# Strassen's scheme for the features of token blocks 0 and 1 in a float32 attention and gated-FFN kernel

## The chip, the cores and the metric

The kernel runs on one core of one Trainium2 chip. The metric is device time in microseconds (us) of one execution; a median of several executions is given. TensorE (PE) multiplies matrices and loads stationary operands beside it (PEld); VectorE (DVE), ScalarE (ACT) and GpSimd (POOL) work on tiles in SBUF; SyncE (SP) issues most of the DMA transfers, ACT some.

## The reference

Two sequences of 2048 tokens, 2048 channels, float32. Each token is normalised; from the normalised x come q, k, v (512 each), the router's q (16) and the bottleneck z (64 experts x 8):

```python
xn  = (x - mean) / sqrt(var + 1e-5)
q, k, v = split(xn @ Wqkv + bqkv)                    # 2048 -> 3 x 512
att = softmax(q @ k.T / sqrt(512)) @ v               # per sequence
gate = scatter(softmax(top_16(xn @ Wq.T @ keys.T)))  # 64 experts
z   = (xn @ A.T).reshape(.., 64, 8) * gate[..., None]
out = x + att @ Wo + bo + 2 * z.reshape(.., 512) @ B.T
```

## The kernel before

Every product of float32 matrices is made of three passes: each operand is split into a rounded high part (`split_hi`, line 126, ACT) and the rest (`split_lo`, line 129, DVE), and `product` (line 132) runs low x high, high x low, high x high.

The 4096 tokens are eight blocks of T = 512; two blocks make a pair. First all blocks get their "features" (12 tiles of 128 rows: q, k and z, made with weights stationary and x moving, 128x512) and their "values" (v and the router's 16 columns, in two halves of VH = 264 columns, x stationary and weights moving, 128x264). Then come scores, softmax and values (lines 1154 to 1316), then the output product (line 1466).

Blocks 0 and 1 are computed directly. `first_block` (line 336) loads block 0's rows, normalises, turns and splits them, and makes its values. `ftile` (line 548) makes one of block 0's 12 feature tiles: 16 chunks of channels x 3 passes = 48 matmuls. Then `values` (line 313) and 12 more calls of `ftile` do block 1; `norm` (line 261) normalises its x, which comes turned from memory (`xT`). Row statistics of the next blocks (`stats_steps`, line 212) run beside.

Pairs 1, 2 and 3 use a scheme of Strassen's kind: for a pair, the two blocks are the columns, the two halves of channels the inner dimension and the two halves of features the rows of a 2 x 2 product, which takes seven products of half size instead of eight. The products are the phases P1, P2, P6, P5, P3, P7, P4 (`phase`, line 801), each six feature pieces of 8 chunks x 3 passes = 24 matmuls and a value piece. P1 + P2 is the first block's first half; the others need sums of x (`sum_steps`, line 673) and sums of weights (`four_sums`, line 572, four GpSimd instructions), which are made once, beside the features of blocks 0 and 1, and stored in DRAM (`sq_d` for features, `sv_d` for values).

The weights of a piece are fetched by `fetch` (line 619) two pieces ahead: a load by SP into one of three buffers (`r_pw`), a high part on ACT and a low part on DVE into one of three pairs (`r_ph`). Results go to DRAM through `store` and `flush` (line 167), on SP's queue.

Each engine takes its instructions in a fixed order, which a planner lays down when the program is built. `behind(...)` holds a step's place in that order behind a named instruction. An SP transfer whose data isn't ready holds up the transfers behind it.

Of the kernel before, what the change touches and what calls it, by code (L numbers as in the profile page):

```python
# [62 lines left out]
def attn_ffn_kernel(ctx: ExitStack, tc, x, xT, wq, wv, wob, bqk, bv, bo, keysT, out):  # L63
# [68 lines left out]
    def product(ps, st, mv, first, end):  # L132

        for n, (a_, b_) in enumerate(PASSES):
            last["pe"] = nc.tensor.matmul(  # L135
                ps, st(a_), mv(b_), start=first and n == 0, stop=end and n == 2
            )
# [35 lines left out]
    r_xh = big(*range(22))  # L173
    r_xs = big(22, 23, 24)
    r_mb = big(25, 26)
    r_ev = big(27, 28, 29)
    r_xc = Ring(sb, "H7", "H8", "B30", "B31")
    r_wu = Ring(sb, "B34", "B35", "G8", "G9", "B36", "B32", "B33")
# [82 lines left out]
    def norm(i, mb):  # L261
        xn = []
        for c in range(NCH):
            xc = r_xc([P, T], F32, "xc")
            nc.sync.dma_start(xc, xT[c * P : (c + 1) * P, i * T : (i + 1) * T])
            nc.vector.tensor_tensor(xc, xc, mb[:, 0, :], ALU.subtract)
            nc.vector.tensor_tensor(xc, xc, mb[:, 1, :], ALU.mult)
            xh = r_xh([P, 2, T], FR, "xh")
            split_hi(xh[:, 0, :], xc)
            split_lo(xh[:, 1, :], xc, xh[:, 0, :])  # L270
            xn.append(xh)
        return xn

# [39 lines left out]
    def values(i, xn, steps):  # L313
        qr = router_in()
        for h in range(2):
            ps = [acc() for t in range(NT)]
            for c2 in range(NCH // 2):
                with behind(*(["ev"] if h == 1 and c2 else [])):
                    wh = wv_piece(h, c2)
                for cc in range(2):  # L320
                    c = 2 * c2 + cc
                    for t in range(NT):
                        sl = slice(t * P, (t + 1) * P)
                        product(
                            ps[t][:, :VH], lambda a: xn[c][:, a, sl], lambda b: wh[:, b, cc, :],
                            c == 0, c == NCH - 1,
                        )
                if h == 1:
                    with behind("sp", "pe", "dve"):
                        steps[c2]()  # L330
            flush()
            for t in range(NT):
                values_out(i, t, h, r_ev, qr, ps[t])
        return qr

    def first_block():


        xs0 = [r_xs, r_xs, r_xs] + [big(j) for j in range(16, 21)]
        xn = [r_xh([P, 2, T], FR, "xh") for c in range(NCH)]  # L340
# [32 lines left out]
        def turn(t, g0=0, g1=NCH // 4):  # L373
            sl = slice(t * P, (t + 1) * P)
            for g in range(g0, g1):
                pt = acc((0, 1, 2, 6)[g])
                for j in range(4):
                    c = 4 * g + j
                    k = (c % 8) * P
                    nc.tensor.transpose(pt[:, j * P : (j + 1) * P], rows[t][c // 8][:, k : k + P], ident)  # L380
                for part in range(2):
                    for j in range(4):
                        hi, lo = (xn[4 * g + j][:, a, sl] for a in range(2))
                        pj = pt[:, j * P : (j + 1) * P]
                        if part == 0:
                            split_hi(hi, pj)
                        else:
                            last["row"] = split_lo(lo, pj, hi)

        r_w0 = Ring(sb, "h0", "h1", "h2", "h3", "B25", "B26", "B32", "B33")  # L390

        def mul(ps, wh, t, c2):
            sl = slice(t * P, (t + 1) * P)
            for cc in range(2):
                c = 2 * c2 + cc
                product(
                    ps[:, :VH], lambda a: xn[c][:, a, sl], lambda b: wh[:, b, cc, :],
# [66 lines left out]
        for c2 in range(N2):  # L464
            w = wv_piece(1, c2)
            for t in range(NT):
                mul(ps[t], w, t, c2)
        for t in range(NT):
# [60 lines left out]
    def feature_out(i, f, ps, gx, u=None):  # L529
        kind, n = divmod(f, ND)  # L530
        if kind < 2:
            ev = r_ev([P, T], F32, "ev")
# [6 lines left out]
        else:  # L539
            zt = r_ev([P, T], F32, "zt")  # L540
# [7 lines left out]
    def ftile(i, f, xn, gx, then=None):  # L548
        ps = acc()
        kind, dc = divmod(f, ND)  # L550
        fh, n = divmod(dc, 2)
        whole = []
        for ch in range(2):
            w = r_wu([P, HC, P], F32, "wu")
            last["sp"] = nc.sync.dma_start(w.rearrange("p k f -> p (k f)"), wq[fh, ch, 2 * kind + n])
            whole.append(w)
            for c4 in range(2):
                ws = w[:, 4 * c4 : 4 * c4 + 4, :]
                wh = r_wh([P, 2, 4, P], FR, "wh")
                last["hi"] = split_hi(wh[:, 0], ws)  # L560
                last["dve"] = split_lo(wh[:, 1], ws, wh[:, 0])
                for cc in range(4):
                    c = ch * HC + 4 * c4 + cc
                    product(
                        ps, lambda a: wh[:, a, cc, :], lambda b: xn[c][:, b, :],
                        c == 0, c == NCH - 1,
                    )
        flush()
        feature_out(i, f, ps, gx)
        return whole  # L570

    def four_sums(w00, w01, w10, w11, dst):
# [6 lines left out]
        with behind("store"):  # L579
            for k, w in enumerate((w11, w00, w10, w01)):  # L580
                nc.sync.dma_start(dst(k), w)
# [9 lines left out]
    def value_sums(m, w):  # L591
        four_sums(
            w[0, 0], w[0, 1], w[1, 0], w[1, 1],
            lambda k: sv_d[k][m // 2][:, 2 * (m % 2) : 2 * (m % 2) + 2, :],
        )
# [9 lines left out]
    GROUPS = ((10, 11, 12, 13), (16, 17, 18, 19), (20, 21, 0, 1), (2, 3, 4, 5))  # L605
    T_SLOTS = (14, 15, 30, 31, 22, 23, 24, 36, 34, 35, 32, 33)
    PAIRS = range(1, NB // 2)
# [4 lines left out]
    }  # L612
    pieces = [
        (j, ph, it, g)
        for j in PAIRS for ph in PHASES for it in ITEMS[ph] for g in range(2 if it == "V" else 1)
    ]
    ready = {}

    def fetch(n):
# [4 lines left out]
        w = WHERE[ph]  # L624
        if it == "V":
# [5 lines left out]
        ws = r_pw(shape, F32, "pw")  # L631
        last["sp"] = nc.sync.dma_start(ws, src)
        hi, lo = (r_ph(shape, FR, "pw") for a in range(2))
# [53 lines left out]
    def beside(j, ph):  # L687
# [3 lines left out]
        s0, s1 = stat_steps.get(2 * j + 2), stat_steps.get(2 * j + 3)  # L691
        if ph == "P1":
            t3 = sum_steps(j, nc.vector, b01, b11, b01, ALU.subtract)
            n10, n01, n11 = x_steps(j, *b10), x_steps(j, *b01), x_steps(j, *b11)
            if j > PAIRS[0]:
                return [], mixed(split_steps(j, "P2", *b10), n01[1], n11[1], t3)
            l = [n10[0][:3], n10[0][3:] + n01[0][:1] + n11[0][:1]]
            return (
                l + [n01[0][k : k + 1] + n11[0][k : k + 1] for k in range(1, NCP)],
                mixed(n10[1], split_steps(j, "P2", *b10)) + mixed(n01[1], n11[1]),  # L700
            )
        if ph == "P2":
            t3 = sum_steps(j, nc.vector, b01, b11, b01, ALU.subtract) if j == PAIRS[0] else []
            return [], mixed(
                t3, sum_steps(j, nc.vector, b00, b01, b00, ALU.add), split_steps(j, "P6", *b00)
            )
# [43 lines left out]
    XU, YU, XV, YV = {}, {}, {}, {}  # L750

    def phase_out(j, ph, it, ps, qr, gx):
# [31 lines left out]
        for n, p in t_of:  # L784
# [6 lines left out]
            elif ph == "P5":  # L791
                nc.vector.tensor_tensor(y_at(n), x_at(n), p, ALU.add)  # L792
            elif ph == "P3":
# [7 lines left out]
    def phase(j, ph, n):  # L801
# [6 lines left out]
        i = 2 * j + (ph in ("P3", "P7"))  # L808
        for m, it in enumerate(ITEMS[ph]):
# [26 lines left out]
            if it == NFP - 2:  # L836
# [4 lines left out]
                gx = {2 * h + k: gate(gfs[i], 2 * h + k) for k in range(2)} if ph in ("P2", "P3", "P7", "P4") else {}  # L841
# [7 lines left out]
            now = steps[m * len(steps) // 7 : (m + 1) * len(steps) // 7]  # L849
            for st in now[0] if now and not callable(now[0]) else now:  # L850
                with behind("sp", "pe", "dve"):
                    st()
# [159 lines left out]


    xn, qr = first_block()
    tile_of = lambda fp, fh: ND * (fp // 2) + 2 * fh + fp % 2
    for i in range(2):
        if i:
            s2 = stats_steps(2, r_xs, 1024, mbs)
            qr = values(i, xn, s2)
        nxt, gx, held, vsum = None, {}, {}, None  # L1020
        pairs = [(0, True), (1, False), (2, True), (3, False), (4, True), (5, False)]
        if i:
            pairs = [(1, True), (0, False), (3, True), (2, False), (5, True), (4, False)]
        order = [(fp, fh, summed) for fp, summed in pairs for fh in range(2)]
        todo = {}
        if i == 0:
            s1 = stats_steps(1, r_xs, 1024, mbs)
            todo = {3 + k: s1[2 * k : 2 * k + 2] for k in range(4)}
            todo |= {7: s1[8:9], 8: s1[9:]}
        else:  # L1030
            s3, q = stats_steps(3, r_xs, 1024, mbs), x_steps(1, 0, 0)
# [687 lines left out]
```

## Time and profile before

| | |
|---|---|
| median of three runs | 2607.29 us (2605.17 to 2610.37) |
| profiled execution, its own time | 2610.36 us |
| its span, first to last instruction | 2608.6 us |
| busy PE / DVE / ACT / POOL | 2587.2 / 1910.3 / 924.8 / 520.0 us |
| block 0's features | 72.8 to 204.4 us |
| block 1's values | 204.4 to 251.9 us |
| block 1's features | 251.9 to 383.8 us |
| moved by DMA | 608.08 MB, 233 GB/s on average |
| granted TensorE clock | 0.999 |

A row of a group gives line, engine, operation, output <- inputs, sizes and count, then busy time and the mean length of one in ns, then the idle time of the engine just before these instructions and what ended it. Names of tiles: xh is a split x tile of blocks 0 and 1, wh a split weight tile, wu and ws loaded weights, pw a weight piece of the phases, t a split operand of the phases. "L127" and "L130" are the lines of the two split helpers, whoever calls them.

### The profile page before, as it was taken

The numbers are of one execution on the slowest core, as the hardware profiler recorded it, in microseconds if no ns is written. First come the engines' busy times: TensorE is split into PE (matmuls) and PEld (weight loads), VectorE is DVE, ScalarE is ACT, GpSimd is POOL, SyncE is SP. The second block draws the span as 40 slices with busy tenths as digits, with TensorE's granted clock in tenths as the row PEclk, the third lists the DMA queues.
The fourth block names the chain that finished last, engine by engine and source line by source line (L and its number), as shares of the span: only waits on it lengthen the run. The fifth ranks groups of instructions, "written<-read, shape, count | busy, mean of one in ns | idle before, by whom it ended". The sixth has DMA issues, their size and how long they took to land. (4 is left out here: it accounts for less than half of the span.)

```text
span 2608.6 us, 34456 instructions
## 1 busy us (share of the span) xinstructions
PE 2587.2 (99%) x12690; PEld 2186.9 (84%) x12690; DVE 1910.3 (73%) x2688; ACT 924.8 (35%) x1377; POOL 520.0 (20%) x318
## 2 busy tenths in 40 slices
PE   8999999999999999999999999999999999999999
PEld 7889888888888888888887888878878888888887
DVE  6557639867878677687668869688598676797675
ACT  4223323323333233343335546354364222332221
POOL 2311520001000010000000000000012665576654
PEclk9999999999999999999999999999999999999999
DMA  6667775668536684577899798889888545565552
GB/s 237 227 249 270 269 265 204 206 205 272 168 130 223 214 276 139 163 246 275 311 316 310 250 342 283 266 316 316 274 302 292 174 156 163 189 214 174 174 167 100
DMA packets 326649, 608.08 MB, mean 233 GB/s; under 512 B 27672, under 2 KB 150608, under 8 KB 326480
## 3 DMA queue, kind: packets, MB, share of 16 engines
q1 hardware_dynamic: 313520, 575.99, 65.1%
q10 hardware_dynamic: 12960, 29.89, 3.4%
q8 instruction: 100, 1.64, 0.3%
q14 instruction: 69, 0.57, 0.1%
HBM read 450.42 MB, written 155.35 MB: 232 GB/s over the span
## 5 line engine op out<-in xcount | busy, mean ns | idle before, releaser
L135 PE MATMUL acc<-t,pw 128*128 128x512 f32 x3024 | 693.4, 390 | 0.0
L135 PEld LDWEIGHTS acc<-t,pw 128*128 128x128 f32 x3024 | 565.5, 188 | 117.3
L1466 PE MATMUL acc<-wb,s 128*128 128x512 f32 x2688 | 609.4, 389 | 0.0
L1466 PEld LDWEIGHTS acc<-wb,s 128*128 128x128 f32 x2688 | 504.7, 188 | 104.6
L1450 POOL TENSOR_TENSOR xo<-xo,bo_bc 128x512 f32<-128x512 f32 x128 | 207.4, 1627 | 893.2 <-DMA bo_bc<-in_bo 588.8
L135 PE MATMUL acc<-ph,vt 128*128 128x512 f32 x1536 | 377.9, 391 | 0.9 <-ACT ot L1311 0.5
L135 PEld LDWEIGHTS acc<-ph,vt 128*128 128x128 f32 x1536 | 288.5, 188 | 63.5 <-issue 2.4
L1172 PE MATMUL acc<-qt,kt 128*128 128x512 f32 x1344 | 334.2, 391 | 2.8 <-ACT sp L1182 1.5
L127 ACT CAST pw<-pw 128x1024 fp32r<-128x1024 f32 (+1 forms) x168 | 177.8, 1059 | 351.6 <-PE acc L135 246.3
L1172 PEld LDWEIGHTS acc<-qt,kt 128*128 128x128 f32 x1344 | 251.6, 188 | 58.5 <-DVE qt L130 2.2
L130 DVE TENSOR_TENSOR pw<-pw 128x1024 fp32r<-128x1024 f32 (+1 forms) x168 | 213.0, 1268 | 74.3 <-ACT pw L127 73.2
L135 PE MATMUL acc<-xh,wh 128*128 128x512 f32 x1152 | 263.7, 390 | 0.0
L135 PEld LDWEIGHTS acc<-xh,wh 128*128 128x128 f32 x1152 | 215.6, 188 | 45.0
L127 ACT CAST s<-xz 128x1024 fp32r<-128x1024 f32 x112 | 118.0, 1055 | 374.9 <-PE acc L1466 310.7
L135 PEld LDWEIGHTS acc<-pw,t 128*128 128x128 f32 x2016 | 245.9, 188 | 4.2 <-DVE yv L792 2.2
L135 PE MATMUL acc<-pw,t 128*128 128x264 f32 x2016 | 247.0, 284 | 2.4 <-DVE yv L792 1.8
L130 DVE TENSOR_TENSOR s<-xz,s 128x1024 fp32r<-128x1024 f32 x112 | 174.0, 1556 | 44.7 <-ACT s L127 44.7
L130 DVE TENSOR_TENSOR wh<-wu,wh 128x512 fp32r<-128x512 f32 x96 | 81.7, 868 | 99.2 <-ACT wh L127 97.0
L545 POOL TENSOR_TENSOR zt<-zt,g 128x512 f32<-128x512 f32 x24 | 39.8, 1668 | 498.9 <-DMA g<-gd 272.6
L1455 DVE TENSOR_TENSOR xo<-xo,acc 128x512 f32<-128x512 f32 x128 | 86.9, 680 | 51.1 <-PE acc L1466 25.4
L130 DVE TENSOR_TENSOR t<-xq,t 128x1024 fp32r<-128x1024 f32 x84 | 107.1, 1281 | 19.0 <-ACT t L127 18.7
L127 ACT CAST t<-xq 128x1024 fp32r<-128x1024 f32 x84 | 88.2, 1051 | 89.9 <-PE acc L135 38.2
(166 smaller groups left out, 2479.8 us busy)
## 6 DMA issues: line engine op xcount, KB each, us to landing
vt<-v_d SPq DMA_DIRECT2D x128, 512.0 KB, 5.3
kt<-kp_d SPq DMA_DIRECT2D x224, 256.0 KB, 5.8
pw<-sq_d SPq DMA_DIRECT2D x72, 512.0 KB, 4.1
xo<-in_x SPq DMA_DIRECT2D x128, 256.0 KB, 3.3
xz<-oz_d SPq DMA_DIRECT2D x64, 512.0 KB, 4.4
out_y<-xo SPq DMA_DIRECT2D x128, 256.0 KB, 2.5
pw<-in_wq SPq DMA_DIRECT2D x54, 512.0 KB, 4.0
wu<-in_wq SPq DMA_DIRECT2D x48, 512.0 KB, 5.8
```

What stands on the lines that cost most here:

```text
L127: return nc.scalar.copy(hi, src)
L130: return (eng or nc.vector).tensor_tensor(lo, src, raw(hi), ALU.subtract)
L135: last["pe"] = nc.tensor.matmul(ps, st(a_), mv(b_), start=first and n == 0, stop=end and n == 2)
L545: nc.gpsimd.tensor_tensor(zt, zt, gx[n], ALU.mult)
L1172: last["pe"] = nc.tensor.matmul(ps, st[:, d, a, :], mv[c][:, d, :], start=not more and d == 0 and i == 0, stop=d == 1 and i == 2, skip_gro ...
L1450: nc.gpsimd.tensor_tensor(xs, xs, bo_bc[q // (NB // 2 * NH), c], ALU.add)
L1455: nc.vector.tensor_tensor(xs, xs, ps, op)
L1466: nc.tensor.matmul(ps, st[a_][:, kk, sl], mv[b_], start=not more and kk == 0 and n == 0, stop=kk == ND - 1 and n == 2, skip_group_check=more,)
```

## The change

Pair 0 (blocks 0 and 1) now runs in the scheme too, in an order of its own.

- `features` makes block 0's first half of features from the two half-channel products, P1 and P2, in 12 pieces of 24 matmuls. The accumulator after P1 is copied to `XU` (P1 is used again later), then P2 is added into the same bank (`more=True` only tells the build that the bank goes on), and the sum is written out as q, k or z.
- `values_by_half` makes block 1's values directly, by halves of channels (Q, R), eight pieces of 48 matmuls of 128x264, on `r_pw`/`r_ph` as all pieces.
- `third` makes P3 in the order `MIXED`, and keeps the result in `WU`. Then the phases P6, P5, P7, P4 run for pair 0 without value pieces. In P5 the kept P3 is added to finish block 1's first half.
- Block 0's x is rejoined from its parts (`whole`), and pair 0's sums of x (`t3`, `t2`, and those of P6) run on DVE.
- The sums of feature weights: sets 0 and 2 whole (128x1024, `set_load`, `set_sums`, `set_out`), the other four in eight parts (128x512, `part_load`, `part_sums`, `part_out`), loaded anew into two rings of two buffers each, `r_hs`: B29 and B9 for parts 0, 1, 3, 5, 7; B27 and B28 for parts 2, 4, 6. The last part is stored while `third` runs, which needs it for its last piece. Sums of value weights move into P6, P5, P7 and P4.
- Block 1's row statistics run beside block 0's second value half; those of block 2 beside `third`, of block 3 beside P5, pair 1's x tiles beside P7 and P4.
- Buffers of x, of the phases and of the weights are laid out anew. All later work stays.

```diff
-    def product(ps, st, mv, first, end):
+    def product(ps, st, mv, first, end, more=False):
...
-    PAIRS = range(1, NB // 2)
+    PAIRS = range(NB // 2)
...
+    MIXED = (0, 2, 4, 1, 3, 5)
     pieces = [
+        (0, "F", 2 * p + f1, ch) for p in range(NFP // 2) for ch in range(2) for f1 in range(2)
+    ]
+    pieces += [(0, ph, h, g) for ph in "QR" for h in range(2) for g in range(2)]
+    pieces += [(0, "P3", it, 0) for it in MIXED]
+    pieces += [(0, ph, it, 0) for ph in ("P6", "P5", "P7", "P4") for it in range(NFP)]
+    pieces += [
         (j, ph, it, g)
-        for j in PAIRS for ph in PHASES for it in ITEMS[ph] for g in range(2 if it == "V" else 1)
+        for j in PAIRS[1:] for ph in PHASES for it in ITEMS[ph] for g in range(2 if it == "V" else 1)
     ]
...
             elif ph == "P5":
                 nc.vector.tensor_tensor(y_at(n), x_at(n), p, ALU.add)
+                if j == 0:
+                    w = WU[n // 2][:, n % 2, :]
+                    feature_out(i1, ND * (n // 2) + n % 2, w, gx, y_at(n), w)
...
+    def features():
...
+        for k, (_, _, fp, ch) in enumerate(pieces[:12]):
+            if ch == 0:
+                tiles[fp] = acc()
+            ps, w = tiles[fp], ready.pop(k)
...
+            for c in range(HC):
+                product(
+                    ps, lambda a: w[a][:, c * P : (c + 1) * P], lambda b: xn[ch * HC + c][b],
+                    c == 0 and ch == 0, c == HC - 1, ch == 1,
+                )
+            fetch(k + 2)
+            flush()
+            if ch == 0:
+                if fp % 2 == 0:
+                    XU[0, fp // 2] = r_xu([P, 2, T], F32, "xu")
+                nc.scalar.copy(XU[0, fp // 2][:, fp % 2, :], ps)
+            else:
+                feature_out(0, ND * (fp // 2) + fp % 2, ps, gx)
...
+    r_hs = big(29, 9), big(27, 28)
+    PARTS = [(fp, k) for fp in (4, 1, 3, 5) for k in range(2)]
+    RINGS = (0, 0, 1, 0, 1, 0, 1, 0)
...
+    def part_sums(n):
+        held["part", n] = four_sums(*(held[n, "part", fh, ch] for fh in range(2) for ch in range(2)))
+
+    def part_out(n):
+        fp, k = PARTS[n]
+        for a, w in enumerate(held["part", n]):
+            nc.sync.dma_start(sq_d[a][fp][:, k * T : (k + 1) * T], w)
...
+    beside_F = {
+        0: stat_steps[1][-2:-1],
+        1: stat_steps[1][-1:] + [lambda: set_load(0)],
+        2: [lambda: set_sums(0)],
+        3: x01[0],
+        5: [lambda: set_load(2), lambda: set_out(0)] + x01[1][:1],
+        6: [lambda: set_sums(2)] + x01[1][1:3],
+        7: x01[1][3:] + [L[0]] + x11[0],
+        8: [S_[0]] + x11[1][:1],
+        9: [lambda: set_out(2)] + x11[1][1:3],
+        10: [O[0], L[1]] + b0[:2] + q_[:1] + x11[1][3:],
+        11: [S_[1]] + b0[2:] + q_[1:2],
+    }
...
+    beside_V = {
+        ("Q", 0, 0): q_[2:] + [L[2], O[1]],
+        ("Q", 0, 1): [S_[2], L[3]] + t3[:2] + b1[:2],
+        ("Q", 1, 0): [O[2], S_[3]] + b1[2:] + t3[2:],
+        ("Q", 1, 1): [L[4], O[3]] + r_[:2],
+        ("R", 0, 0): [S_[4], L[5]] + r_[2:],
+        ("R", 0, 1): [O[4], S_[5]] + t2[:2],
+        ("R", 1, 0): [O[5], L[6], lambda: state.update(q=router(qr1))] + t2[2:],
+        ("R", 1, 1): [S_[6], L[7]],
+        0: [S_[7], O[6], lambda: state.update(w=choose(state["q"]))] + st[:2],
+        1: [O[7]] + p6[:1] + st[2:5],
...
+    }
...
+    n = features()
...
+    n = values_by_half(n)
+    n = third(n)
     r_ev = big(27, 28, 29, 9)
...
+    for m, ph in enumerate(("P6", "P5", "P7", "P4")):
+        a, b, c = value_sums(m)
+        n = phase(0, ph, n, {0: [a], 2: [b], 4: [c]})
+    for j in PAIRS[1:]:
         for ph in PHASES:
```

## The prediction

> **What bounds the kernel now.** I read the engine shares first, then TensorE's own waits, then the busy time by stage.
>
> ```profile
> PE 2587.2 (99%) x12690; PEld 2186.9 (84%) x12690; DVE 1910.3 (73%) x2688; ACT 924.8 (35%) x1377; POOL 520.0 (20%) x318
> ...
> L135 PE MATMUL acc<-xh,wh 128*128 128x512 f32 x1152 | 263.7, 390 | 0.0
> ```
>
> TensorE is busy for 99% of the span, and the group that the change is about (features of blocks 0 and 1, tile names xh and wh) never waited. The waits of TensorE alone add up to about 17 us in 2608.6; nothing but matmul count matters unless a new wait appears. By stage (columns: busy time of PE, its weight loads, DVE, ACT, POOL, then granted clock, DMA share, GB/s):
>
> ```profile
> 43.50:72.80 29.30, 29.30 (x240) 29.30 (x241) 13.54 (x22) 10.81 (x20) 6.11 (x4) 1.00 0.35 110
> 72.80:204.40 131.60, 131.60 (x584) 108.75 (x583) 76.56 (x133) 40.28 (x71) 33.45 (x14) 1.00 0.72 256
> 204.40:251.90 47.50, 46.98 (x386) 46.55 (x385) 34.56 (x63) 14.66 (x32) 0.68 (x1) 1.00 0.78 268
> 251.90:383.80 131.90, 131.90 (x586) 108.68 (x585) 73.61 (x115) 37.38 (x65) 58.91 (x27) 1.00 0.74 259
> ```
>
> These are: block 0's values (most of them), block 0's features, block 1's values, block 1's features. In the features DVE is busy 58% of the time, the DMA engines 72 to 74%, so two bounds stand not far behind TensorE. Spacing of matmuls: between 117.12 and 160.75 us TensorE ran 192 of 128x512, 43.63/192 = 0.2272 us each (the 390 ns in the group's row is the pipelined length, not the spacing); from 43.50 to 72.80 it ran 240 of 128x264, 0.122 us each.
>
> **What is removed.** Before, 2 blocks x 12 tiles x 16 chunks x 3 passes = 1152 matmuls of 128x512. After: `features` 12 pieces x 8 x 3 = 288, `third` 6 x 24 = 144, and four phases x 6 x 24 = 576, together 1008. The values keep 768 of 128x264. So 144 go: 144 x 0.2272 = 32.7 us. The one wait of TensorE in that stretch (0.5 us at 231 us, on ACT, in block 1's values) belongs to a loop that is replaced; I count 0.5 us more. Ceiling: 33.2 us.
>
> **What is added or moved, and where it hides.** With no new wait the new stage runs: features 12 x 24 x 0.2272 = 65.4 us, values of block 1 384 x 0.122 = 46.8, `third` 32.7 (so 145 us), then P6, P5, P7, P4 at 32.7 each.
>
> Block 1's row statistics (16 BATCH_NORM_STATS2 at 0.68 us, eight 512 KB loads issued by ACT) move into block 0's second value half. DVE is busy 13.5 of 29.3 us there and DMA 0.35: nothing on the path. Were that cover gone, 11 us of DVE would lie ahead of the first weight split. Blocks 2 and 3's statistics and pair 1's x tiles move into `third`, P5, P7 and P4; the work of each phase on DVE is about 24 to 28 us of 32.7 (P7: six weight splits, four operand splits and eight norm steps at 1.13 us spacing, twelve evacuations at 0.6: 27.5), so it fits; ACT has under half of its time taken. Pair 1's P1 loses this work but had no wait of TensorE: nothing gained.
>
> The 145 us are dense. DVE instructions with both inputs in SBUF: about 62 of 128x1024 (26 weight splits, 16 norm steps, 12 operand splits, 8 sums) at 1.13 us spacing = 70; 16 halves of `whole` at 0.60 = 10; eight value splits 3: 83 us. GpSimd's weight sums: eight of 128x1024 at 2.39 (undisturbed rows at 320.02 and 322.49 us) = 19, and 32 of 128x512 at 1.29 = 41: 60 us. Before, the same sums were spread over 311 us. How the two engines meet:
>
> ```profile
> 302.10 7.69 POOL L575 TENSOR_TENSOR ws<-ws 128x528 f32<-128x528 f32 x1 [7.73 <-DMA ws<-in_wv]
> 302.70 3.49 DVE L130 TENSOR_TENSOR t<-xq,t 128x1024 fp32r<-128x1024 f32 x3
> 306.11 2.49 DVE L130 TENSOR_TENSOR wh<-wu,wh 128x512 fp32r<-128x512 f32 x4
> 313.33 1.33 POOL L578 TENSOR_TENSOR ws<-ws 128x528 f32<-128x528 f32 x1
> 2049.23 1.29 POOL L1450 TENSOR_TENSOR xo<-xo,bo_bc 128x512 f32<-128x512 f32 x1 [5.08 <-DMA xo<-in_x]
> 2070.41 2.29 POOL L1450 TENSOR_TENSOR xo<-xo,bo_bc 128x512 f32<-128x512 f32 x1
> ```
>
> A GpSimd sum took 1.33 us alone, 7.69 behind seven DVE instructions in a row, and 2.29 for a 1.29 in the output stage. But the mean of the existing sums of 128x1024 is only 2.55 to 2.78 us against 2.39 alone, because DVE has gaps there: by that row 60 us become 67 of 145, no wait at all. The Trainium skill, page "SBUF — State Buffer", section "Who interferes with whom", speaks against the change: a DVE instruction with two SBUF inputs and a GpSimd instruction that reads SBUF block each other, whichever comes second waiting for the first to finish. By it 83 + 60 = 143 us must go one after another in 145. Counted piece by piece from the end of the third feature piece, where the first sums begin, to the end of the second piece of `third`, 131 us are due in 107, of which 5 find nothing to do: a backlog of 29 us. The last sum's store, load and split need another 10 or so, and the piece that uses it begins three pieces, 16.4 us, later: 22 us late. I take a value between 0 and 22, by the 2.29 us row, in this way.
>
> Sums in parts go load, sum, store. Parts 0, 1, 3, 5, 7 share buffers B29 and B9, so they follow each other. From the end of feature piece 8 (116 us) to the time when the last weights of P3 must have landed (about 208 us: that piece begins at 212) there are 92 us; less one load of 5 us, 87 us for five rounds, 17.4 each. A round: loads 5.8 (median of wu<-in_wq), four sums, store 4.2. With 1.29 us sums it is 15.2 and fits; with 2.29 it is 19.2, five of which are 9 us too long. Who waits: SP's stores stand at the head of its queue until GpSimd is done, and behind them stand the weight loads of the next pieces and the stores of values, whose two buffers DVE needs. So a late sum becomes a late weight split. I take 9 us (bounds 0 and 22).
>
> DMA: in the 145 us there are 26 weight pieces (13.7 MB), loads for sums 10.5, their stores 12.6, x tiles and rows 8.4, outputs and gates 8: about 53 MB, of which 4 can be fetched before 72.8 us. 49/145 = 338 GB/s. The trace's best:
>
> ```profile
> 280.00:290.00 10.00, 10.00 (x46) 8.28 (x45) 4.78 (x10) 2.08 (x4) 0.00 (x0) 1.00 1.05 407
> 1360.00:1390.00 30.00, 30.00 (x134) 24.86 (x133) 18.59 (x33) 12.46 (x24) 0.00 (x0) 1.00 1.03 364
> ```
>
> By 364 GB/s, full over 30 us, the 49 MB take 135 us: hidden. The same page, section "A bandwidth-pool intuition that's wrong (but worth ruling out)", gives some 358 GB/s for memory to a core, an estimate of 137 us (and 148 with none fetched ahead, 3 us over). I take nothing, 3 us as the bound.
>
> A stall also costs clock. After 1.54 us of idle at 1411 us the row of 1410 to 1415 shows 0.93 granted and the next five 0.73: (0.07 + 0.27) x 5 = 1.7 us; after 1.80 us idle at 563 the clock stayed at 1.00. For several short waits I add 2 us, and 1 us for waits on accumulator banks (1.8 us at 563 was such a one).
>
> **Sum.** 2610.36 (the profiled execution; span 2608.6 and 1.8 around it) - 33.2 + 9 + 2 + 1 = 2589.2. The median of the runs is 2607.29, 3.1 below, so 2586.
>
> **Rivals.** (a) All hidden: waits 0 to 6 us, 2574 to 2580. For it: DVE and GpSimd overlap with only 10% loss in today's rows, and loads may run ahead; against it, the dense 145 us. (b) GpSimd serial with DVE and stores late in several places: waits of 20 to 38 us, 2594 to 2612; for it the 7.69 us row, against it that a waiting TensorE lets GpSimd catch up, so one backlog isn't paid twice. (c) Slower: the ring of part buffers. Five rounds 33 us too long need 17.4 + 33.2/5 = 24 us a round, so (24 - 10)/4 = 3.5 us for each sum of 128x512; from there on the change loses. At 4 us a sum, 26 a round, waits of 43 us give 2617. For it the single 7.69; against it the means of the output stage's sums of this size, 1627 to 1783 ns, where DVE is busy too. (d) That the matmuls are not fewer is excluded: the count follows from the loops.
>
> **How the numbers follow.** Likeliest, waits of 6 to 20 us: 0.45, 2580 to 2594. (a) 0.27, (b) 0.15, (c) 0.13. About 0.2% (5.2 us) is what a measurement of this kernel can tell from no change. The lower half of (b) still is faster, its upper half no change: faster 0.79, same 0.08, slower 0.13. Range: down to 2574 (ceiling of the gain), up to 2609, which leaves (c) and a little of both edges out.
>
> **What would show it.** Right: 1008 matmuls in place of 1152; the four phases before pair 1 at 32.7 us each; TensorE waits of some us behind weight splits or casts between 140 and 230 us, with SP waiting on GpSimd; sums of 128x512 at 1.7 to 2.5 us; pair 1 and all after it shifted unchanged. Wrong: the sums at 1.3 to 1.5 and no wait (a), or waits in P6 to P4 or in features, where I count none, or block 0's values longer than 29.3 us.

## The result, and the profile after

The changed kernel takes 2616.95 us (median of 6 runs, 2614.61 to 2621.78), the kernel before 2607.68 us in the same comparison (6 runs, 2605.17 to 2610.37): a ratio of 1.0037, interval 1.0024 to 1.0050. It is 9 us slower. The prediction was 2586 us, and a range that ended at 2609: wrong in sign and outside the range.

The page of the changed kernel (engine shares) and two of its groups:

```profile
PE 2564.3 (98%) x12546; PEld 2166.3 (83%) x12546; DVE 1986.6 (76%) x2692; ACT 927.4 (35%) x1327; POOL 552.1 (21%) x340
...
L1132 DVE TENSOR_TENSOR xq<-xh 128x512 f32<-128x512 f32 x16 | 20.3, 1325 | 0.0
...
L542 POOL TENSOR_TENSOR hs<-hs 128x512 f32<-128x512 f32 x8 | 14.9, 1862 | 0.6
```

The 144 matmuls are gone (12690 - 12546). They should have taken 32.7 us of TensorE's busy time with them, from 2587.2 to 2554.5; it is 2564.3, so the remaining matmuls ran 9.8 us slower. And TensorE's idle time, the span less its busy time, rose from 2608.6 - 2587.2 = 21.4 to 2614.2 - 2564.3 = 49.9 us: 28.5 more. Together -32.7 + 9.8 + 28.5 = 5.6, the difference of the spans. L1132 is the adding that rejoins block 0's x (`whole`), L542 the last of the four instructions of a part sum; both are slower than I had put them.

Where it happened, by stage (busy time of PE, weight loads, DVE, ACT, POOL; granted clock, DMA share, GB/s): block 0's features, block 1's values, P3 (`third`), the first of the four phases.

```profile
73.56:139.89 66.33, 66.33 (x297) 54.63 (x295) 47.62 (x65) 21.32 (x30) 20.60 (x12) 1.00 0.92 318
139.89:207.33 67.44, 51.59 (x386) 50.80 (x385) 55.23 (x46) 19.26 (x27) 40.52 (x24) 0.90 0.71 240
207.33:250.35 43.02, 36.29 (x152) 29.54 (x151) 27.82 (x66) 13.82 (x22) 6.65 (x5) 0.92 0.92 312
250.35:283.00 32.65, 32.65 (x146) 26.97 (x145) 30.95 (x31) 11.63 (x13) 12.45 (x7) 1.00 0.67 227
```

The features take 66.3 us as counted, without a wait. Block 1's values take 67.4 instead of 46.8, of which 15.9 are idle and the rest a clock of 0.90; P3 takes 43.0 instead of 32.7. These two lose 31 of the gain's 33 us. In the values GpSimd is busy for 40.5 us and DVE for 55.2, and the DMA engines are less busy (0.71) than in the stages around them.

TensorE's waits, and then the matmuls that stood behind the longest of them (start, length, idle before and what ended it):

```profile
PE acc L135 <- DVE t L130: 18.5, 7, 7.3
PE misc L499 <- DVE wk L491: 6.7, 1, 6.7
...
PE acc L135 <- DVE pw L130: 3.1, 2, 2.2
PE acc L135 <- DVE qr L938: 2.7, 1, 2.7
```

```profile
148.55 22.88 PE L135 MATMUL acc<-pw,t 128*128 128x264 f32 x165 [5.24 <-DVE t L130]
178.77 7.38 PE L135 MATMUL acc<-pw,t 128*128 128x264 f32 x48 [7.35 <-DVE t L130]
...
231.04 0.66 PE L499 MATMUL misc<-ident,wk 128*128 128x128 f32 x2 [6.73 <-DVE wk L491]
```

t is a split operand of x. What stood in front of it is in the timeline of DVE, GpSimd and SP between 158 and 179 us (start, length):

```profile
158.83 5.79 DVE L1132 TENSOR_TENSOR xq<-xh 128x512 f32<-128x512 f32 x4
164.55 2.35 DVE L130 TENSOR_TENSOR pw<-pw 128x1056 fp32r<-128x1056 f32 x1
166.81 6.85 DVE L1132 TENSOR_TENSOR xq<-xh 128x512 f32<-128x512 f32 x4
173.59 2.35 DVE L665 TENSOR_TENSOR xq<-xq 128x1024 f32<-128x1024 f32 x2
176.23 1.26 DVE L130 TENSOR_TENSOR pw<-pw 128x1056 fp32r<-128x1056 f32 x1 [0.30 <-ACT pw L127]
177.41 3.43 DVE L130 TENSOR_TENSOR t<-xq,t 128x1024 fp32r<-128x1024 f32 x2
...
168.00 1.74 POOL L542 TENSOR_TENSOR hs<-hs 128x512 f32<-128x512 f32 x1
169.70 1.74 POOL L541 TENSOR_TENSOR hs<-hs 128x512 f32<-128x512 f32 x1
171.52 1.59 POOL L542 TENSOR_TENSOR hs<-hs 128x512 f32<-128x512 f32 x1
...
160.69 9.40 SPq L1170 DMA_DIRECT2D sq_d<-hs  x4
170.18 0.39 SPq L620 DMA_DIRECT2D pw<-in_wv  x1
```

The four adds at 166.81 take 6.85 us, 1.7 each, where 0.60 was due; a GpSimd sum beside them takes 1.7 too, where 1.29 was due. So one of each goes by in 1.7 us. At the spacings that they have alone (0.60, and 1.36 between two sums at 187.8 us, with DVE idle) they would take 2.0 us one after the other: they take turns, with little overlap. And SP stood for 9.4 us at the stores of part sums (L1170), with a weight load (L620) behind them. That load's cast and DVE's own backlog end together, at 176.2 and 175.9 us. Later in this stage DVE does stand idle for weights whose loads are late, 2.0 us at 182.8 and 2.3 us at 190.1. From this trace alone either could be the cause; the experiments have to tell.

### The profile page after: what moved, and what is told of

Read it like the earlier page. It is cut to its first block, busy times and chain, and to the rows that moved or that the text cites. A ratio compares the mean times of both kernels' runs of the same rounds, so it can differ in the third digit from the quotient of the medians.

```text
span 2614.2 us, 34207 instructions
## 1 busy us (share of the span) xinstructions
PE 2564.3 (98%) x12546; PEld 2166.3 (83%) x12546; DVE 1986.6 (76%) x2692; ACT 927.4 (35%) x1327; POOL 552.1 (21%) x340
## 5 line engine op out<-in xcount | busy, mean ns | idle before, releaser
L135 PE MATMUL acc<-t,pw 128*128 128x512 f32 x3744 | 863.0, 391 | 7.5 <-DVE t L130 5.3
L135 PEld LDWEIGHTS acc<-t,pw 128*128 128x128 f32 x3744 | 702.9, 189 | 155.9 <-DVE t L130 7.0
L127 ACT CAST pw<-pw 128x1024 fp32r<-128x1024 f32 (+1 forms) x218 | 230.4, 1058 | 461.4 <-PE acc L135 286.9
L130 DVE TENSOR_TENSOR pw<-pw 128x1024 fp32r<-128x1024 f32 (+1 forms) x218 | 284.0, 1303 | 109.4 <-ACT pw L127 107.8
L135 PE MATMUL acc<-pw,t 128*128 128x264 f32 x2400 | 298.8, 286 | 16.9 <-DVE t L130 13.2
L135 PEld LDWEIGHTS acc<-pw,t 128*128 128x128 f32 x2400 | 296.8, 190 | 19.6 <-ACT yv L936 7.5
L130 DVE TENSOR_TENSOR t<-xq,t 128x1024 fp32r<-128x1024 f32 x108 | 141.2, 1314 | 22.8 <-ACT t L127 22.6
L127 ACT CAST ph<-sp 128x512 fp32r<-128x512 f32 x128 | 79.4, 620 | 111.8 <-PE acc L135 111.1
L224 DVE BATCH_NORM_STATS2 st<-xs 128x6 f32<-128x512 f32 x128 | 84.8, 683 | 42.3 <-DMA xs<-in_x 41.8
L1633 POOL TENSOR_TENSOR xo<-xo,u 128x512 f32<-128x512 f32 x64 | 111.6, 1773 | 20.7 <-DVE u L1631 20.5
```

The source lines that it names most:

```text
L127: return nc.scalar.copy(hi, src)
L130: return (eng or nc.vector).tensor_tensor(lo, src, raw(hi), ALU.subtract)
L135: last["pe"] = nc.tensor.matmul(ps, st(a_), mv(b_), start=first and n == 0, stop=end and n == 2, skip_group_check=more,)
L224: nc.vector.bn_stats(st[:, parts, :], xt[:, h * 512 : (h + 1) * 512])
L1633: nc.gpsimd.tensor_tensor(xo[q, t, a, 1], xo[q, t, a, 1], v, ALU.add)
```

## The experiments

Theory 1: the part sums on GpSimd hold DVE, and DVE's operand splits come late. Rival, the prediction's own mechanism: the sums' loads and stores hold SP's queue and the weights come late. Other rivals: the order of steps (gates, norms), and DVE's amount of work. The kernel before took 2607.7 to 2608.9 us (medians) in all comparisons below.

**The part sums left out.**

```diff
-        held["part", n] = four_sums(*(held[n, "part", fh, ch] for fh in range(2) for ch in range(2)))
+        held["part", n] = [held[n, "part", fh, ch] for fh in range(2) for ch in range(2)]
```

> Leaves out the 32 GpSimd sums of the eight weight parts (128x512); their loads and stores stay, so the weights of P3 to P7 for four of six sets are not sums. Theory 1, GpSimd's sums make DVE late (its 128x512 rejoining of x takes 1.4 to 1.7 us in place of 0.60 beside them, and the operand splits that TensorE waits for stand behind it): the stretch of block 1's values falls from 67 us to about 50, TensorE's waits on operand splits there from 13 us to under 5, the time from 2617 to 2597 to 2603. Theory 2, DVE has too much work of its own there: the rejoining falls to 0.6 us but the waits stay over 10 us and the time over 2610. Theory 3, DMA traffic and the stores at the head of SP's queue: no change beyond 5 us, since a store still waits for its load.

Measured: 2596.99 us, ratio 0.9954 (0.9940 to 0.9969), 20 us below the changed kernel. Page, group and the stage of block 1's values:

```profile
PE 2561.2 (99%) x12546; PEld 2163.2 (83%) x12546; DVE 1959.7 (76%) x2692; ACT 927.7 (36%) x1327; POOL 496.4 (19%) x308
...
L1132 DVE TENSOR_TENSOR xq<-xh 128x512 f32<-128x512 f32 x16 | 10.1, 687 | 0.0
...
140.82:189.88 49.06, 47.38 (x386) 46.80 (x385) 37.85 (x48) 19.85 (x28) 0.00 (x0) 1.00 0.94 323
```

Block 1's values take 49.1 us instead of 67.4. DVE runs the same 2692 instructions in 26.9 us less (1986.6 - 1959.7), though no sum was DVE's. Not all of that is the sums'. Up to the end of P4 DVE runs the same 449 instructions in both kernels (the changed one first; DVE's busy time and count, then clock and DMA):

```profile
0.00:390.00 390.00, 309.96 (x449) 0.96 0.80 282
...
0.00:373.50 373.50, 288.19 (x449) 0.97 0.84 295
```

The difference is 21.8 us; the other 5 us arise after 1757 us, long after the last part sum. The 32 sums cost GpSimd 552.1 - 496.4 = 55.7 us, 1.74 each; 32 x 1.29 would be 41.3. So the sums lost GpSimd 14 us and DVE 22. One wait is not theirs: 4.4 of the 6.7 us for block 1's gates stay without them.

**The sums kept, most of their transfers left out.** Six of the eight parts reuse buffers that are already loaded, no part sum is stored, and the phases read unsummed weights.

```diff
+        if n not in (0, 2):
...
+                    held[n, "part", fh, ch] = held[2 * RINGS[n], "part", fh, ch]
+            return
...
-            nc.sync.dma_start(sq_d[a][fp][:, k * T : (k + 1) * T], w)
```

> Keeps all GpSimd sums of the parts but leaves out six of eight parts' loads and all their stores (about 15 MB); the sums are made again on the first loads, and the phases read unsummed weights. Theory 1 (GpSimd against DVE): TensorE still waits 8 us or more for operand splits in block 1's values, time 2610 to 2620; the sums may even start earlier, in the features, as no load holds them. Theory 3 (DMA and SP's queue): these waits go, the stretch falls to about 50 us and the time to 2597 to 2603.

Measured: 2626.26 us, ratio 1.0064 (1.0049 to 1.0079). Nothing on SP waits for a part sum here, and it is slower still, beyond the ranges of both theories. TensorE's waits:

```profile
PE acc L135 <- DVE t L130: 30.7, 5, 12.1
```

The sums, no longer paced by loads and stores, come closer together; the waits on operand splits grow from 18.5 to 30.7 us. From 110 to 146 us sums of 128x512 and DVE instructions of 128x1024 go by at one of each in 2.24 us, where their spacings alone add up to 1.13 + 1.36 = 2.5: the same taking of turns. SP's queue isn't needed for the loss; what it costs by itself this run doesn't tell, because the sums press harder on DVE as well.

**Block 1's gates three pieces later; its norms one or two pieces earlier.** Two kernels, one move each.

```diff
-        2: [lambda: gfs.update({1: gates(1, state["w"])})] + p6[1:2] + st[5:8],
+        2: p6[1:2] + st[5:8],
...
-        5: st[13:-2],
+        5: [lambda: gfs.update({1: gates(1, state["w"])})] + st[13:-2],
```

> Moves only the step that turns block 1's gates (two TensorE transposes, which wait for DVE's selection) from the third piece of P3 to its last. If the 6.7 us wait of TensorE at 224 us and the slower clock after it (0.68 between 230 and 240 us, some 2.4 us) are a cost of their own, the time falls by 7 to 9 us to 2608 to 2610. If DVE is late anyway and TensorE would wait for the next split instead, it falls by less than 3 us.

```diff
-        5: [lambda: set_load(2), lambda: set_out(0)] + x01[1][:1],
-        6: [lambda: set_sums(2)] + x01[1][1:3],
-        7: x01[1][3:] + [L[0]] + x11[0],
-        8: [S_[0]] + x11[1][:1],
-        9: [lambda: set_out(2)] + x11[1][1:3],
-        10: [O[0], L[1]] + b0[:2] + q_[:1] + x11[1][3:],
+        4: x01[1][:2],
+        5: [lambda: set_load(2), lambda: set_out(0)] + x01[1][2:] + x11[0],
+        6: [lambda: set_sums(2)] + x11[1][:1],
+        7: [L[0]] + x11[1][1:3],
+        8: [S_[0]] + x11[1][3:],
+        9: [lambda: set_out(2)],
+        10: [O[0], L[1]] + b0[:2] + q_[:1],
```

> Moves the eight normalising steps of block 1's x one to two feature pieces earlier (into a time when DVE and GpSimd have gaps, 94 to 109 us), nothing else. If DVE's backlog from 110 us on makes the first wait in block 1's values (5.2 us, and the clock of 0.78 to 0.88 after it), that wait goes and the time falls by 5 to 9 us, to 2608 to 2612. If the sums' contention inside the values makes all of it, the first wait shrinks by 2 us or less and the time stays within 3 us.

Measured: 2618.24 (1.0035, 1.0022 to 1.0047) and 2618.53 (1.0035, 1.0022 to 1.0048): no gain from either. The wait that each aimed at went, the gates' 6.7 and the first 5.2 us, and others took its place, behind operand splits, a weight split and copies of value results. While DVE was late, neither order helped.

**The sums in halves of 128x256.**

```diff
-        tt = nc.gpsimd.tensor_tensor
+            for q in range(2):
+                sl = slice(q * n, (q + 1) * n)
+                nc.gpsimd.tensor_tensor(o[:, sl], a[:, sl], b[:, sl], op)
```

> Leaves nothing out: each GpSimd part sum of 128x512 is made as two of 128x256, 64 instructions instead of 32. Theory 1 (a DVE instruction with two SBUF inputs waits for the end of the GpSimd instruction that it meets, so what is lost depends on the length of the GpSimd instruction): a halved sum holds DVE half as long, the mean of the rejoining adds (128x512, 1325 ns in the changed kernel, 687 without part sums) falls to about 1000 ns, TensorE's waits on operand splits from 21 to about 12 us, time 2608 to 2613. Theory 2 (the two engines share a bandwidth, so that the loss goes by the bytes): mean stays at 1.3 us, time 2615 to 2619. A third outcome: twice as many GpSimd instructions mean twice as many turns that DVE gives away; the loss per DVE instruction stays at about 1 us, more of them meet one, and the time is 2617 to 2625.

Measured: 2624.79 us, ratio 1.0060 (1.0043 to 1.0077). Page and groups:

```profile
PE 2564.5 (98%) x12546; PEld 2164.8 (83%) x12546; DVE 1974.7 (75%) x2692; ACT 927.5 (35%) x1327; POOL 577.2 (22%) x372
...
L544 POOL TENSOR_TENSOR hs<-hs 128x256 f32<-128x256 f32 x64 | 75.1, 1210 | 47.2 <-DMA hs<-in_wq 46.5 <-issue 0.6
...
L1139 DVE TENSOR_TENSOR xq<-xh 128x512 f32<-128x512 f32 x16 | 12.7, 850 | 0.0
```

DVE's loss fell as theory 1 has it: 1974.7 - 1959.7 = 15.0 us for 26.9 by the pages (14 for 22 up to the end of P4), a rejoining add 850 ns for 1325. But GpSimd has twice as many instructions that can be held: its sums are busy for 75.1 us (L544). In the changed kernel the same measure, over L539 to L542, is 56.8. The shortest half took 0.72 us, so 64 of them alone would be 46 us, 5 more than the whole sums; the rest, 29 us for 15, is loss to DVE. And here the prediction's mechanism does show: DVE, no longer the later of the two, idled for value weights (2.8 us at 179.9, 3.7 us at 188.5) whose loads stood behind stores of part sums on SP (6.9 and 5.6 us, from 166.7 and from 176.8 us). Fewer microseconds on DVE, and yet slower. The time lies in the range of the third outcome, but its reason does not hold: DVE gave away fewer microseconds, not more.

**The rejoining adds in pairs** (128x1024, 9 instructions for 16, the same bytes).

```diff
+        both = whole_of[ch * NCP + cp]
+        if both:
+            nc.vector.tensor_tensor(t, raw(both[0]), raw(both[1]), ALU.add)
-        for k in range(2):
+        for k in range(0 if both else 2):
```

> Leaves nothing out: block 0's x parts lie in pairs of chunks, so a rejoining add is one of 128x1024 instead of two of 128x512: 9 instructions for 16, the same bytes. Theory 1 (about 1.0 us lost for each DVE instruction that meets a GpSimd one, whatever its size): 7 instructions fewer, 4 to 7 us less on DVE, waits on operand splits 14 to 17 us for 21, time 2610 to 2614. Theory 2 (loss by bytes): 2616 to 2618.

Measured: 2621.83 us, ratio 1.0048 (1.0033 to 1.0063). A miss for both theories: I had put a fixed 1.0 us on each DVE instruction that meets a sum, so that fewer would lose less. DVE's busy time hardly fell (1984.8 for 1986.6), and no run shows why the kernel is slower than with the adds unpaired.

**The part sums on DVE.**

```diff
-        held["part", n] = four_sums(*(held[n, "part", fh, ch] for fh in range(2) for ch in range(2)))
+        held["part", n] = four_sums(*(held[n, "part", fh, ch] for fh in range(2) for ch in range(2)), nc.vector)
```

> Leaves nothing out: the 32 part sums run on DVE instead of GpSimd, at the same places of the order. Theory 1 (meeting of DVE and GpSimd costs about 1.0 us for each DVE instruction): DVE gets 32 x 0.60 = 19 us more work and loses no time to GpSimd, about 30 us less, so the values of block 1 take 48 to 58 us instead of 67; time 2600 to 2611. Rival (DVE is full in that stretch whoever blocks it; added work is added wait, and a sum waits on its load at the head of DVE's queue): values of 65 us or more, time 2615 to 2630.

Measured: 2606.52 us, ratio 0.9988 (0.9981 to 0.9995), 10.4 us below the changed kernel. Page:

```profile
PE 2561.3 (98%) x12546; PEld 2163.8 (83%) x12546; DVE 1978.6 (76%) x2724; ACT 927.3 (36%) x1327; POOL 493.1 (19%) x308
```

DVE does 32 instructions more and is busy for 8 us less. Its own 32 sums cost it 19 us (0.60 spacing each), GpSimd's 32 had cost it 22. With both edits, pairs and sums on DVE:

> Leaves nothing out: the two edits together, part sums on DVE and rejoining adds in pairs. Theory 1: with nothing of GpSimd's part sums left to meet, the pairs save only the fixed cost of 7 instructions, below 1 us; the time is that of the sums on DVE alone less 0 to 2 us, 2599 to 2611. Rival (bytes, DVE full): the same as the sums on DVE, 2615 to 2630.

2604.98 us, ratio 0.9985 (0.9976 to 0.9994): with the sums on DVE the pairs do no harm, and 1.5 us of gain lies inside the intervals.

**Sums on DVE, and the two moves again; then the value weights' sums on DVE too.** Four kernels: part sums on DVE with both moves; the same with the 16 sums of value weights (128x528, beside P6 to P4) on DVE; that with pairs; and all 48 sums on DVE without the moves.

```diff
-            v["s"] = four_sums(w[0, 0], w[0, 1], w[1, 0], w[1, 1])
+            v["s"] = four_sums(w[0, 0], w[0, 1], w[1, 0], w[1, 1], nc.vector)
```

> Leaves nothing out: the 32 part sums on DVE, and block 1's x tiles normalised one to two pieces earlier, and its gates moved from the third piece of P3 to the last. With the sums on DVE alone TensorE still waited 3.7 + 3.2 us in block 1's values and 5.6 us for the gates. Theory 1 (with GpSimd off its back DVE has room, so order can now be mended): these three fall to 4 us in all, the clock returns to 0.997, time 2592 to 2602. Rival (DVE is full there in any order, as when either move was made with the sums on GpSimd): the waits move to operand splits, time 2604 to 2610.

> Leaves nothing out: as the kernel with part sums on DVE and the two moves, and the 16 sums of value weights (128x528, beside P6 to P4) on DVE too. In P5 DVE's 128x1024 weight splits took 1.9 to 2.35 us where these sums ran, and 1.2 elsewhere. Theory 1: 16 x 0.6 = 10 us of DVE work added, some 16 us of blocking gone, TensorE's waits in P6 to P4 (about 8 us) fall by 2 to 5, time 2 to 5 us below the former. Rival (these waits hang on late weight loads and on the number of DVE instructions per phase): no change within 2 us or slower.

> Leaves nothing out: as the former, and the rejoining adds in pairs (128x1024). Theory 1: fewer instructions of the same bytes without anything to meet, 0 to 2 us below the former.

> Leaves nothing out: part sums and sums of value weights on DVE, without the two moves. Against the kernel with part sums alone on DVE (2606.5): theory 1, 2 to 5 us less (2601 to 2605); rival, 2605 to 2610.

Measured: 2598.62 (0.9965, 0.9951 to 0.9978), 2595.92 (0.9959, 0.9946 to 0.9971), 2596.34 (0.9953, 0.9940 to 0.9966) and 2603.38 us (0.9977, 0.9968 to 0.9985). The moves, which each alone gained nothing beside GpSimd's sums, are together worth 8 us without them, in both pairs of kernels (2606.5 to 2598.6; 2603.4 to 2595.9); whether both moves together would have gained beside GpSimd's sums was not run. The value sums on DVE bring about 3 us in both, each time less than the intervals tell apart. Pairing brought nothing. (The slowed splits that the second expectation puts in P5 lie in P4.) Page and waits of the second:

```profile
PE 2561.2 (99%) x12546; PEld 2163.9 (83%) x12546; DVE 1979.8 (76%) x2740; ACT 928.2 (36%) x1327; POOL 457.7 (18%) x292
```

```profile
PE acc L135 <- DVE t L130: 10.0, 5, 3.7
...
PE acc L135 <- DVE pw L130: 1.8, 1, 1.8
```

It leaves nothing out and beats both kernels: 12.6 us below the kernel before, 21 below the changed one. DVE does 48 instructions more than in the changed kernel and is busy for 6.8 us less.

**What is left of the 33 us.** With all 48 sums left out and the two moves, and then with the rejoining left out of DVE's work too:

```diff
-            nc.vector.tensor_tensor(t[:, k, :], raw(hi), raw(lo), ALU.add)
+            nc.scalar.copy(t[:, k, :], raw(hi))
```

> Leaves out the 32 part sums and the 16 sums of value weights (weights are used and stored unsummed; all transfers stay); norms early and gates late as in the kernel of 2595.9 us, whose DVE does these 48 sums. If the 20 us still missing there to 2575 (all hidden) are DVE's crowding, 29 us less on DVE give back most of it: 2576 to 2586. If they are something else (transfers, banks, loads held up on SP's queue), it stays at 2590 to 2597, near the 2597.0 without the moves.

> As the former, and block 0's x is not rejoined: ScalarE copies the high part (16 of 128x512), the low part is left out, so DVE has 10 us less just ahead of the operand splits that TensorE waited for. DVE crowding: 2575 to 2583, waits on operand splits in block 1's values below 1 us. Otherwise: as the former within 2 us.

Measured: 2586.12 (0.9910, 0.9893 to 0.9926) and 2590.87 us (0.9932, 0.9918 to 0.9947). The first 29 us of DVE's work (48 x 0.60; 24.3 by the pages) are worth 10; the next 10 us are worth nothing, rather the contrary, and the second time lies in neither of its ranges. In the profiled execution of the first (2591.2 us) TensorE is idle 6.6 us more than in the kernel before (2589.4 - 2561.4, for 21.4) and its matmuls are 6.9 us slower (2561.4 for 2554.5), so what is left is of both kinds. What TensorE waits for in P3 there is a weight split that is late because its load is:

```profile
PE acc L135 <- DVE pw L130: 3.6, 2, 2.7
...
213.88 1.22 DVE L130 TENSOR_TENSOR pw<-pw 128x1024 fp32r<-128x1024 f32 x1 [3.57 <-ACT pw L127]
...
212.81 1.04 ACT L127 CAST pw<-pw 128x1024 fp32r<-128x1024 f32 x1 [3.21 <-DMA pw<-sq_d]
```

**The part stores off SP's queue.** They are issued by GpSimd, with the sums whole and in halves on GpSimd; and, with all sums on DVE and both moves, by GpSimd or by ScalarE.

```diff
-            nc.sync.dma_start(sq_d[a][fp][:, k * T : (k + 1) * T], w)
+            nc.gpsimd.dma_start(sq_d[a][fp][:, k * T : (k + 1) * T], w)
```

> Leaves nothing out: the 32 stores of part sums are issued by GpSimd, which makes the sums, instead of SP, so no weight load stands behind a store that waits for a sum. In the changed kernel such a store stood at the head of SP's queue from 160.7 to 170.2 us, the value weights behind it were cast at about 176.2, and DVE came free at 175.9: two chains that end together. If both are needed (DVE held by the sums, and SP by the stores): moving the stores alone leaves DVE's chain, waits in block 1's values fall by 0 to 4 us, time 2611 to 2618. If SP's queue is the true cause and DVE only happens to end with it: waits fall by 8 or more, 2600 to 2609.

> Leaves nothing out: the stores on GpSimd's queue as in the former, and the part sums in halves of 128x256. In halves with the stores on SP, DVE lost 15 us to the sums instead of 27, but GpSimd took 20 us more for them, SP's queue was held, and DVE idled for value weights; 2624.8. Two chains: with SP free of it, DVE's smaller loss comes through, 2603 to 2613. If DVE's time is what counts alone, SP played no part and the halves stay slow: 2618 to 2626.

> Leaves nothing out: all 48 sums on DVE, norms early, gates late (2595.9 us with the stores on SP), and the part stores on GpSimd's queue. If weight loads held on SP behind these stores are what is left (with no sums at all TensorE still waited 2.7 us in P3 for a weight part whose load was late): 2587 to 2594. If not: 2594 to 2598.

> As the former, with the part stores issued by ScalarE, which then stands behind DVE's sums before it casts the next weights: as the former if ScalarE has slack (32% busy), 2598 to 2610 if its casts are late next.

Measured: 2623.39 (1.0060, 1.0045 to 1.0075), 2635.97 (1.0113, 1.0096 to 1.0130), 2600.56 (0.9975, 0.9965 to 0.9984) and 2602.19 us (0.9981, 0.9974 to 0.9987). All four are slower than their counterparts with the stores on SP, by 5 to 11 us (the smallest of these, the third, at the edge of what the intervals tell apart). The first three lie above every range that I had put; the fourth lies in its range for late casts on ScalarE, and TensorE waits there 4.1 us for a weight split and 2.4 us for a copy on ScalarE, where it waited 1.8 us and nothing with the stores on SP. The timeline of the first: TensorE's longest wait, then ScalarE, DVE and GpSimd ahead of it.

```profile
184.74 15.45 PE L135 MATMUL acc<-pw,t 128*128 128x264 f32 x105 [14.23 <-DVE t L130]
...
173.28 1.07 ACT L127 CAST pw<-pw 128x1056 fp32r<-128x1056 f32 x1
...
175.57 4.48 DVE L665 TENSOR_TENSOR xq<-xq 128x1024 f32<-128x1024 f32 x2
179.98 2.31 DVE L130 TENSOR_TENSOR pw<-pw 128x1056 fp32r<-128x1056 f32 x1
182.21 3.52 DVE L130 TENSOR_TENSOR t<-xq,t 128x1024 fp32r<-128x1024 f32 x2
```

ScalarE casts these weights at 173.3 us, 6.7 us before DVE comes to them: no weight is late, DVE alone is, and TensorE waits for 14.2 us. So DVE's chain is sufficient without SP's. What SP's chain alone costs stays open: this run, like the one without part traffic, also makes DVE busier (1990.8 and 1995.5 us, for 1986.6). That the stores on GpSimd's queue make it worse is a second effect, below under the hardware.

## Why the prediction was wrong

By its own steps:

- **144 x 0.2272 = 32.7 us of matmuls go.** Right: 144 records fewer, and in stages without a wait the lengths are as counted (features 66.3 for 65.4; the first phase 32.65 for 32.7).
- **Waits of 9 us from late sums (bounds 0 and 22).** This step failed, in its size and in its place. TensorE idled for 28.5 us more. The step took the meeting of DVE and GpSimd as a cost to GpSimd alone: sums of 2.29 instead of 1.29 us, and DVE at its own pace of 1.13 and 0.60. The sums took 1.74, less than I put, and DVE lost 22 us, which I had at nothing. I also followed the delay along SP's queue, from a late store to a late weight, and never along DVE's own order, where the operand splits of Q and R stand behind the rejoining adds.
- **The rule that was weighed.** By the Trainium skill, page "SBUF — State Buffer", section "Who interferes with whom", a DVE instruction with two SBUF inputs and a GpSimd instruction that reads SBUF block each other, the second waiting for the first. The runs side with it: adds and sums at 1.7 us each beside each other, for 0.60 and 1.29 alone. By that rule I had counted a backlog of 29 us up to P3's second piece and a last part 22 us late; TensorE idled for 15.9 us up to there. I scaled the count down to 9 by rows of a stage where DVE had gaps (2.29, and means of 2.55 to 2.78 for 2.39). A mean over a stage with gaps says nothing of one with none. Even 22 us would have made only 2599: the next two points, a slower clock and waits elsewhere, are the rest.
- **SP's ring of part buffers.** In the changed kernel it is seen (9.4 us at the head of the queue), and it ends 0.3 us apart from DVE's chain. Taken away it gains nothing, in two ways (2626.3 and 2623.4, each with more loss on DVE); it shows alone where the sums are halved. So DVE's chain is enough for the waits, and SP's is a second one that ends with it in this place; its own share is not isolated.
- **Clock 2 us, banks 1 us.** Mis-sized: the same matmuls were busy for 9.8 us longer. Behind the waits the granted clock was 0.90 in block 1's values and 0.92 in P3, for 1.00 before.
- **No waits in features, P3's gates or P6 to P4.** The prediction counts no wait in these. Right for the features, wrong for the rest: 6.7 us for the gates (DVE, L491), of which 4.4 came without any part sum, and 5.5 us in P7 and P4. With the value weights' sums on DVE the waits in P4 are gone, and one in P7 is longer (3.7 us).
- **DMA hidden.** Not what set the changed kernel's time (a share of 0.71 in its worst stage, 0.92 in the stages on both sides). With no sums at all, one weight of P3 came late (a wait of 2.7 us); whether for bandwidth or for its place in SP's order isn't shown.
- **The rivals.** The time is that of (c), 2617, but not by (c)'s mechanism, which needed sums of 3.5 us and more; they took 1.74. That it came near its number is luck. (b), GpSimd serial with DVE, named the right meeting, and the 28.5 us of added idle time lie within its 20 to 38; the slower clock carries the time beyond its 2612. Against it I had put that "a waiting TensorE lets GpSimd catch up", where the backlog that TensorE waited for was DVE's.

Settled: 20 of the 42 us between an estimate of the time with everything hidden (2607.7 - 32.7 = 2575) and the changed kernel come from GpSimd's part sums, and DVE's loss to them is enough to make TensorE wait. With DVE making all sums, and two steps moved, 21 are got back. Another 10 are the sums' work on DVE (2595.9 to 2586.1, the sums left out). The last 11 stay open: less work for DVE does not bring them, moving the part stores off SP does not, and late weight loads in P3 are a part of it whose size wasn't isolated.

## What to carry to other kernels

Where two-input DVE instructions and GpSimd adds both work on SBUF without gaps, count their times as a sum and ask which engine's queue the loss falls in: adds left to GpSimd can cost DVE as much (22 us here) as doing them itself (19 us). When work is squeezed from 311 into 145 us, durations measured in the loose stage no longer hold for the dense one. Two moves that did not help one by one while DVE was late helped together once it wasn't (8 us here), so cures are to be tried again after the bottleneck has gone.

## What the runs showed of the hardware

- How the loss is shared goes with how the work is cut. Sums of 128x512 lost DVE 22 us and GpSimd 14 to 15; sums of 128x256 lost DVE 14 and GpSimd 29. Cutting the work of one engine moved the loss to that engine here; it didn't remove it.
- The turns are not always one for one. With stores issued by GpSimd between its sums, a DVE instruction was held over two sums. In the kernel with whole sums and stores on GpSimd (timeline of DVE and GpSimd):

```profile
154.64 4.48 DVE L130 TENSOR_TENSOR pw<-pw 128x1056 fp32r<-128x1056 f32 x1 [2.88 <-ACT pw L127]
...
154.88 1.29 POOL L542 TENSOR_TENSOR hs<-hs 128x512 f32<-128x512 f32 x1
156.11 0.56 POOL L1170 DMA_DIRECT2D sq_d<-hs  x1
156.69 1.30 POOL L539 TENSOR_TENSOR hs<-hs 128x512 f32<-128x512 f32 x1
157.92 0.56 POOL L1170 DMA_DIRECT2D sq_d<-hs  x1
```

One split of 1.26 us took 4.48, over two sums and the issues between, and the sums beside it their 1.29 and 1.30: it didn't get its turn after the first sum, as DVE does in the changed kernel. The reverse occurs too: in the kernel with sums in halves, one of 128x256 took 7.0 us, from 140.8 to 147.8 us, while seven DVE instructions went by at their own lengths until DVE had nothing to do, as seven did beside the sum of 7.69 us that the prediction shows. What decides who goes next, no run here shows.
- Each of the three waits of 5.2 to 7.4 us was followed by reduced clock for two rows of 5 us (0.76 and 0.56; 0.50 and 0.83; 0.50 and 0.87), then by 1.00. The first of them (busy time of PE, clock, DMA):

```profile
145.00:150.00 5.00, 1.45 (x6) 0.76 0.86 270
150.00:155.00 5.00, 5.00 (x27) 0.56 0.89 313
155.00:160.00 5.00, 5.00 (x43) 1.00 0.78 257
```

The waits of 0.6 to 2.7 us up to the end of P4 were followed by 1.00; one of 2.0 us at 390.8, just behind it, by 0.83 and 0.82. Block 1's values and P3 together lost 8.4 us to slower matmuls (51.6 for 46.8 and 36.3 for 32.7) beside 22.6 us of idle time, so a wait there cost about a third more than its own length.
